# Shared experts of 512 tokens computed in pieces between the attention's steps

## The chip, the cores and the metric

The kernel runs on one core of a Trainium2 chip. A core has a matrix engine (TensorE, PE in the profile), VectorE (DVE), ScalarE (ACT), GpSimd (POOL) and SyncE (SP), each with an instruction stream of its own; they meet through semaphores. Data live in SBUF (128 partitions) and PSUM (the matmuls' accumulators), and DMA queues move them from and to HBM. The metric is the device time of one launch in microseconds (us): before the change the median of 8 runs is 1922.06 us (1921.56 to 1927.59).

## The reference

Four residual layers follow each other on x (1250 nodes of 512 values), each with a layer norm ahead of it. The change touches the first two; the two behind (a message passing layer with GRU and a KAN layer) only follow.

```python
x = x + gnn(layernorm(x), edges)           # attention over 21,250 edges, 8 heads of 32
x = x + ffn(layernorm(x))                  # router, 2 shared and 64 routed experts
x = x + gnn2(layernorm(x), edges, edge_attr)
x = x + kan(layernorm(x))

# gnn: att = exp(Q[receiver].K[sender]/sqrt(32)), normalised over a receiver's edges
out = relu(segment_sum(att * V[sender])); out = relu(out @ Wa + ba); out = relu(out @ Wf + bf)
return x + out
# ffn
shared = sum_over_2(silu(x @ Wg.T) * (x @ Wu.T) @ Wd.T) / 2
probs = softmax(x @ router_w.T + bias); top_p, top_i = top_k(probs, 6); top_p /= sum(top_p)
# each expert takes at most C = 234 of its tokens, in the order of the tokens
sparse = segment_sum(gate * (silu(t @ w_gate[e].T) * (t @ w_up[e].T)) @ w_down[e].T)
return shared + sparse
```

## The kernel before, in words

Tokens lie in ten tiles of 128 (`NT`), in chunks of 512, 512 and 256 (`CHUNKS`). `xr` keeps the residual stream in SBUF, `hT` the transposed normed tokens. The stages of the span, in us: counting of edges, norm, Q, K and V to 164; attention to 412; a tail to 444; shared experts of chunk 0 and the look-up of places to 491; shared experts of chunk 2 and the first experts' tokens to 515; routed experts to 991; shared experts of chunk 1 and the next norm to 1080; messages, GRU and KAN to the end. Matmuls in f32 are two PE instructions each.

**Attention.** Edges are counted into `cnts` (sender by receiver). A step is one chunk, one half of the heads and one tile b of ten senders: 3 chunks, 2 halves, 10 steps. `scores` (L472) makes four matmuls (L477) into two PSUM buffers `ps` (of three in all), takes the exponent on ACT into `ex` (L482) and multiplies it by the counts on DVE into `wt` (L484). `weighted` (L490) sums V and ones with it on PE (L496). The loop at L534 issues `scores` two steps ahead of `weighted`. After a half, `normalised` (L499) copies the sums to `s` on ACT, and DVE takes the reciprocal (L506) and writes `aggT` (L507).

**What is put between the steps.** At b = 5 of a chunk's first half, `output` (L510) of the chunk before runs whole: L517 and L525 on PE, and on DVE the bias into `o2` (L528; the profile calls it o) and the ReLU into `xr` (L530). Then the generator `route` (L386) gives one part behind each step: statistics of two tiles; `h` on ACT (L182), its transpose on PE (L191) and `hT` on ACT (L192) for each tile; router matmuls (L402) and softmax; top six (L418, L419); one-hot choices `hot` (L431); their sum `sel` (L435); the place of each choice in its expert's list, by matmuls on `sel` and `before` (L440, L441); `hu`, `pos` and `tat` (L449 to L456). The last part issues on POOL's queue one scatter (L459) for each tile and choice, which writes token and gate into the table `tokt` in HBM: 24 for a chunk of four tiles, 12 for the last chunk. The tail, L555 to L557, is `output` and `route` of the last chunk and what is left of the route before it.

**Behind the attention.** `sg` and `sd`, the weights of the shared experts (3 MB), are loaded by SP (L566 to L568) into memory that the attention's tiles held. `order` (L626) is the list of experts by load; SP reads it to address their weights. The program's dependencies let its write wait for the scatters. `shared_experts(*CHUNKS[0])` (L628) makes four pairs of gate and up matmuls (L582), Silu on ACT (L585), their product `sT` on DVE (L586), and for each tile the down matmuls (L590) and the sum into `xr` (L593). SP loads the table back as `tokb` (L631) when the last scatter has landed. Behind the last matmul of that call, `by_place` (L645) and `by_rank` sort the table by 42 small matmuls (L652, L658); `tok` (L676), `gate` and `goal` come from them. `shared_experts(*CHUNKS[2])` (L681) follows. `Tile.load` (L740) sends an expert's weights on SP into one of six buffers `w`, each load behind the one before it and the first behind `tokb`; `Tile.rows` (L750) gathers its tokens on POOL (L206) from `xtab`, to which the route has written `h`; `hidden` and `result` hold the expert matmuls (L764, L781). POOL adds each result to `acc` in HBM (L787). Chunk 1's shared experts run behind the routed experts.

**Memory.** Pools on SBUF's left side open and close in a stack, and pools on its right side in another.

Of the kernel before, what the change touches and what calls it, by code (L numbers as in the profile page):

```python
# [10 lines left out]
F32 = mybir.dt.float32  # L11
BF = mybir.dt.bfloat16
F16 = mybir.dt.float16
I16 = mybir.dt.int16
I32 = mybir.dt.int32
# [7 lines left out]
P = 128  # L23
N = 1250
NT = 10
# [54 lines left out]
def gnn_ffn_kernel(ctx: ExitStack, tc: tile.TileContext, a: dict, out: bass.AP):  # L80
# [21 lines left out]
    early = until_attended.enter_context(tc.tile_pool(name="early", bufs=1))  # L102
    srcf = early.tile([P, ET], F32, name="srcf")
    dstf = const.tile([P, ET], F32, name="dstf")
# [7 lines left out]
    with tc.tile_pool(name="near", bufs=1) as temp:  # L112
# [10 lines left out]
        nc.vector.tensor_reduce(n_far, near, AX.X, OP.add)  # L123
    iot_i = early.tile([P, P], I32, name="iot_i")
    nc.gpsimd.iota(iot_i, pattern=[[1, P]], base=0, channel_multiplier=0)
    iot = const.tile([P, P], F32, name="iot")
    nc.vector.tensor_copy(iot, iot_i)
    iotn = early.tile([P, NP], F16, name="iotn")
    with tc.tile_pool(name="iot_t", bufs=1) as temp:
# [92 lines left out]
    with tc.tile_pool(name="gat", bufs=1) as gw:  # L222
# [88 lines left out]
        with tc.If(far):  # L311
            with tc.tile_pool(name="gat_f", bufs=2) as work, \
                    tc.tile_pool(name="gat_fp", bufs=1, space=PSUM) as psum:
                for j in range(0, NT, 2):
# [10 lines left out]
                    for i in range(2):  # L325
                        nc.vector.scalar_tensor_tensor(
                            cnts[:, j + i], pc[i][:, :NP], 1.0, cnts[:, j + i], op0=OP.mult,
                            op1=OP.add, accum_out=deg[:, j + i:j + i + 1])

        wa = gw.tile([P, HD // P, D], F32, name="wa")  # L330
        nc.sync.dma_start(out=wa, in_=a["Wa"].rearrange("(c p) f -> p c f", p=P))
# [46 lines left out]
        nc.vector.scalar_tensor_tensor(qh, qe, -2.0, qf, op0=OP.mult, op1=OP.add)  # L378

        sel = rt.tile([P, NT, NE], BF, name="sel")  # L380
        before = rt.tile([P, NT + 1, NE], BF, name="before")
# [3 lines left out]

        def route(t0, n, work, psum):  # L386

# [4 lines left out]
            def new(name, *shape, dt=F32):  # L392
                return work.tile([P, n, *shape], dt, name=name, bufs=1)
# [53 lines left out]
            yield  # L447
            hu = new("hu", TOPK, NE)
            nc.vector.tensor_tensor(hu, hot, u[:, :, None, :].to_broadcast([P, n, TOPK, NE]), OP.mult)  # L449
# [5 lines left out]
            tat = work.tile([P, n, TOPK], I32, name="tat", bufs=2)  # L455
            nc.vector.tensor_scalar(tat, past, float(NPOS), None, op0=OP.add)  # L456
            for t in range(n):
                for k in range(TOPK):
                    s = nc.gpsimd.indirect_dma_start(  # L459
                        out=tokt, out_offset=IndirectOffsetOnAxis(ap=tat[:, t, k:k + 1], axis=0),  # L460
                        in_=entry[:, t0 + t, k], in_offset=None)
                    for other in scatters:
                        tc.declare_no_dep(s.ins, other.ins, reason="each place is of one choice")
                    scatters.append(s)

        with tc.tile_pool(name="gat_e", bufs=3) as work, \
                tc.tile_pool(name="gat_o", bufs=2) as owork, \
                tc.tile_pool(name="gat_r", bufs=1) as rwork, \
# [3 lines left out]
            def scores(n0, n, half, b):  # L472

                ps = [psum.tile([P, 2, 512], F32, name="ps") for _ in range(2)]
                for i in range(4):
                    q = slice(i * DK, (i + 1) * DK)
                    nc.tensor.matmul(ps[i // 2][:, i % 2, :n], KT[q, half, b * P:(b + 1) * P],  # L477
                                     QT[q, half, n0:n0 + n], start=True, stop=True)
                wts = []
                for p in ps:  # L480
                    ex = work.tile([P, 2, 512], F32, name="ex")
                    nc.scalar.activation(ex[:, :, :n], p[:, :, :n], AF.Exp, scale=DK ** -0.5)  # L482
                    wt = work.tile([P, 2, 512], F32, name="wt", bufs=6)
                    nc.vector.scalar_tensor_tensor(  # L484
                        wt[:, :, :n], ex[:, :, :n], HUGE,
                        cnts[:, b, None, n0:n0 + n].to_broadcast([P, 2, n]), op0=OP.min, op1=OP.mult)
                    wts.append(wt)
                return wts

            def weighted(n, half, b, wts, acc):  # L490

                for part in range(2):
                    for i in range(4):
                        h = 4 * half + i
                        v = ones[:, :DK] if part else V[:, b, h * DK:(h + 1) * DK]
                        nc.tensor.matmul(acc[part][i * DK:(i + 1) * DK, :n], v, wts[i // 2][:, i % 2, :n],  # L496
                                         start=b == 0, stop=b == NT - 1)
# [12 lines left out]
            def output(n0, n, aggT):  # L510
                o1T = owork.tile([P, DC, 512], F32, name="o1T", bufs=1)
                for f in range(0, DC, 2):
                    p1 = psum.tile([P, 2, 512], F32, name="ps")
                    for i in range(2):
                        fs = slice((f + i) * P, (f + i + 1) * P)
                        for c in range(HD // P):
                            nc.tensor.matmul(p1[:, i, :n], wa[:, c, fs], aggT[:, c, :n], start=c == 0,  # L517
                                             stop=c == HD // P - 1)
                        nc.scalar.activation(o1T[:, f + i, :n], p1[:, i, :n], AF.Relu,
                                             bias=cols[:, C_BA + f + i:C_BA + f + i + 1])  # L520
                for t in range(0, n // P, 2):
                    p2 = psum.tile([P, 2, D], F32, name="ps")
                    for i in range(2):
                        for c in range(DC):
                            nc.tensor.matmul(p2[:, i], o1T[:, c, (t + i) * P:(t + i + 1) * P], wf[:, c],  # L525
                                             start=c == 0, stop=c == DC - 1)
                    o2 = owork.tile([P, 2, D], F32, name="o2", bufs=1)
                    nc.vector.tensor_add(o2, p2, bf[:, None, :].to_broadcast([P, 2, D]))  # L528
                    xs = xr[:, n0 // P + t:n0 // P + t + 2]
                    nc.vector.scalar_tensor_tensor(xs, o2, 0.0, xs, op0=OP.max, op1=OP.add)  # L530

            steps = [(n0, n, half, b) for n0, n in CHUNKS for half in range(2) for b in range(NT)]
            ready, done, acc, aggT, parts = [], None, None, None, iter(())
            for i in range(len(steps) + 2):  # L534
                if i < len(steps):
                    ready.append(scores(*steps[i]))
                if i < 2:
                    continue
                n0, n, half, b = steps[i - 2]
                if b == 0:  # L540
                    acc = [psum1.tile([P, 512], F32, name=f"acc{k}") for k in range(2)]
                    if half == 0:
                        aggT = owork.tile([P, 2, 512], F32, name="aggT")
                weighted(n, half, b, ready.pop(0), acc)
                if b == NT // 2 and half == 0 and done:
                    output(*done)
                    parts = chain(parts, route(done[0] // P, done[1] // P, rwork, psum))
                    done = None
                else:
                    next(parts, None)  # L550
                if b == NT - 1:
                    normalised(n, half, acc, aggT)
                    if half == 1:
                        done = n0, n, aggT
            output(*done)  # L555
            for _ in chain(parts, route(done[0] // P, done[1] // P, rwork, psum)):
                pass  # L557
# [3 lines left out]

    until_moe = ExitStack()
    shared = until_moe.enter_context(tc.tile_pool(name="shared", bufs=1, reuse_waits="tile"))
    sg = shared.tile([P, 2, DC, 2 * FF], F32, name="sg")
    sd = shared.tile([P, 2 * FF // P, D], F32, name="sd")
    for i in range(2):  # L566
        nc.sync.dma_start(out=sg[:, i], in_=a["shared_in"][i].rearrange("(c p) f -> p c f", p=P))
    nc.sync.dma_start(out=sd, in_=a["shared_out"].rearrange("(c p) d -> p c d", p=P))  # L568
    until_edges = ExitStack()
# [27 lines left out]
    with tc.tile_pool(name="moe", bufs=1, side="right") as mw, tc.tile_pool(name="moe_w", bufs=6) as ew:  # L597
        with tc.tile_pool(name="moe_s", bufs=1) as keep, \
# [28 lines left out]

            last = shared_experts(*CHUNKS[0], keep, psum, psum1)  # L628

# [50 lines left out]
            goals(goal.rearrange("p r h -> p (r h)"), pm[:, 2])  # L680
            shared_experts(*CHUNKS[2], keep, psum, psum1)  # L681


# [196 lines left out]
    finishing.close()  # L880
    until_edges.close()
    until_msgs.close()
    until_moe.close()


    with ExitStack() as kan:
# [281 lines left out]
        def new(name, bufs):  # L1168
            return work.tile([P, 2, KC], F32, name=name, bufs=bufs)
# [231 lines left out]
```

## Time and profile before

| | us |
|---|---|
| Median of 8 runs | 1922.06 |
| Profiled execution, its own time | 1922.51 |
| Its span | 1920.8 |
| PE busy | 1815.2 |
| DVE, ACT, POOL busy | 1030.6, 756.7, 441.6 |
| Third norm transpose of chunk 1's route | starts 380.42 |
| Last `weighted` step ends, first L517 of the last chunk | 407.1 |
| First slot matmul of chunk 2 (L440) | 443.46 |
| Scatters of chunk 1, of chunk 2 | 412.4 to 442.2, 448.3 to 463.2 |
| `tokb` issued | 465.46 |
| First gather of an expert's tokens | 494.39 |
| First expert transpose, first expert matmul | 514.30, 515.78 |

A time in this table is a start on its engine from the span's beginning, unless it says otherwise. Busy times of engines overlap, so they do not add up to the span. A stage's own numbers say more than the whole span's: in a window, the idle time of PE is the window's length less its busy time, and the granted clock tells whether busy time was at full speed. A wait is put down to the instruction whose end released it.

### The profile page before, as it was taken

The numbers are of one execution on the slowest core, as the hardware profiler recorded it, in microseconds if no ns is written. First come the engines' busy times: TensorE is split into PE (matmuls) and PEld (weight loads), VectorE is DVE, ScalarE is ACT, GpSimd is POOL, SyncE is SP. The second block draws the span as 40 slices with busy tenths as digits, with TensorE's granted clock in tenths as the row PEclk, the third lists the DMA queues.
The fourth block names the chain that finished last, engine by engine and source line by source line (L and its number), as shares of the span: only waits on it lengthen the run. The fifth ranks groups of instructions, "written<-read, shape, count | busy, mean of one in ns | idle before, by whom it ended". The sixth has DMA issues, their size and how long they took to land. (4 is left out here: it accounts for less than half of the span.)

```text
span 1920.8 us, 20622 instructions
## 1 busy us (share of the span) xinstructions
PE 1815.2 (95%) x7477; PEld 898.3 (47%) x7477; DVE 1030.6 (54%) x1742; ACT 756.7 (39%) x1193; POOL 441.6 (23%) x421
## 2 busy tenths in 40 slices
PE   6999998968999999999989899998999999998999
PEld 4664232334544444444434334333447766664644
DVE  8765859563111111111128365552235987899995
ACT  3214644421022222222212144441116877687772
POOL 0000000434134444444420377761000000000000
PEclk9999999988999999999999999999999999999999
DMA  8000000004399999888864488881110001000000
GB/s 316 5 1 2 1 17 7 23 3 179 130 272 302 279 308 291 246 305 300 296 157 138 130 283 283 287 284 48 49 49 1 1 33 62 5 11 1 11 10 22
DMA packets 68403, 247.24 MB, mean 129 GB/s; under 512 B 11889, under 2 KB 14705, under 8 KB 59189
## 3 DMA queue, kind: packets, MB, share of 16 engines
q1 hardware_dynamic: 29954, 147.65, 20.5%
q0 software_dynamic: 32656, 83.97, 16.6%
q10 hardware_dynamic: 5666, 14.05, 2.0%
q8 instruction: 66, 1.08, 0.2%
q14 instruction: 61, 0.49, 0.1%
HBM read 210.23 MB, written 35.39 MB: 128 GB/s over the span
## 5 line engine op out<-in xcount | busy, mean ns | idle before, releaser
L764 PE MATMUL pg<-w,xT 128*128 128x512 f32 (+4 forms) x752 | 274.9, 595 | 3.9 <-DMA w<-in_experts 3.0
L768 DVE TENSOR_TENSOR gs<-gs,pg 128x256 f32<-128x256 f32 (+2 forms) x76 | 32.0, 421 | 390.6 <-ACT gs L767 390.6
L206 POOL DMA_INDIRECT hg<-ptab,srci x167 | 158.3, 948 | 153.3 <-DVE at L974 90.1
L764 PEld LDWEIGHTS pg<-w,xT 128*128 128x128 f32 (+4 forms) x752 | 105.3, 164 | 161.0 <-issue 158.4
L787 POOL DMA_INDIRECT acc<-y,goal x94 | 140.6, 1495 | 155.5 <-ACT y L785 134.8
L932 PE MATMUL pm<-w1e,eat 128*128 128x512 f32 x334 | 159.1, 614 | 8.8 <-DVE m L934 8.0
L781 PE MATMUL py<-w,gT 128*128 128x512 f32 (+4 forms) x376 | 149.4, 611 | 9.6 <-ACT gT L776 3.3
L1237 PE MATMUL pk<-basis,w1s 128*128 128x256 f32 x640 | 150.0, 381 | 2.1 <-DVE basis L1219 2.1
L1260 PE MATMUL py<-block,basis 128*128 128x512 f32 x320 | 142.8, 607 | 9.3 <-DVE basis L1219 9.3
L934 DVE TENSOR_TENSOR m<-pm,hg 128x1024 f32<-128x1024 f32 x84 | 102.3, 1218 | 83.6 <-PE pm L932 46.7
L935 ACT ACTIVATE m<-m 128x1024 f32<-128x1024 f32 x84 | 88.1, 1050 | 137.2 <-DVE m L934 137.2
L1237 PEld LDWEIGHTS pk<-basis,w1s 128*128 128x128 f32 x640 | 120.1, 190 | 39.8 <-issue 14.8
L1196 DVE SCALAR_TENSOR_TENSOR cube<-held,knots,sq 128x512 f32<-128x512 f32 x180 | 135.3, 754 | 4.4 <-ACT sq L1192 4.1
L1192 ACT ACTIVATE sq<-held,negk 128x512 f32<-128x512 f32 x180 | 127.4, 710 | 24.3 <-DVE cube L1196 24.2
L482 ACT ACTIVATE ex<-ps 128x1024 f32<-128x1024 f32 (+1 forms) x120 | 101.1, 883 | 88.0 <-PE ps L477 65.7
L484 DVE SCALAR_TENSOR_TENSOR wt<-ex,cnts 128x1024 f32<-128x1024 f32 (+1 forms) x120 | 119.6, 1041 | 28.2 <-ACT ex L482 28.2
L767 ACT ACTIVATE gs<-pg 128x256 f32<-128x256 f32 (+2 forms) x76 | 29.1, 383 | 223.6 <-PE pg L764 210.2
L785 ACT ACTIVATE y<-py,gate 128x512 f32<-128x512 f32 (+2 forms) x76 | 52.2, 686 | 159.4 <-PE py L781 122.4
L206 POOL DMA_INDIRECT xg<-xtab,tok x76 | 75.0, 987 | 159.4 <-PE pt L758 121.5
L932 PEld LDWEIGHTS pm<-w1e,eat 128*128 128x128 f32 x334 | 60.0, 192 | 99.2 <-issue 77.0
L1260 PEld LDWEIGHTS py<-block,basis 128*128 128x128 f32 x320 | 62.2, 196 | 86.8 <-issue 71.4
L1203 ACT ACTIVATE right<-cube 128x512 f32<-128x512 f32 x135 | 84.0, 622 | 39.5 <-DVE cube L1196 35.4
(284 smaller groups left out, 2736.4 us busy)
## 6 DMA issues: line engine op xcount, KB each, us to landing
w<-in_experts SPq DMA_DIRECT2D x64, 1536.0 KB, 10.5
eat<-in_edge SPq DMA_DIRECT2D x20, 512.0 KB, 5.8
acc<-zero SPq DMA_DIRECT2D x33, 256.0 KB, 5.1
part<-acc SPq DMA_DIRECT2D x30, 256.0 KB, 5.3
block<-in_w SPq DMA_DIRECT2D x3, 1536.0 KB, 6.2
w1s<-in_w1s ACTq DMA_DIRECT2D x4, 1024.0 KB, 4.9
block<-in_Wih ACTq DMA_DIRECT2D x4, 768.0 KB, 6.8
block<-in_Whh ACTq DMA_DIRECT2D x4, 768.0 KB, 6.4
```

The costliest lines, as they stand in the source:

```text
L206: nc.gpsimd.indirect_dma_start(out=dst, out_offset=None, in_=table, in_offset=IndirectOffsetOnAxis(ap=at, axis=0))
L482: nc.scalar.activation(ex[:, :, :n], p[:, :, :n], AF.Exp, scale=DK ** -0.5)
L484: nc.vector.scalar_tensor_tensor(wt[:, :, :n], ex[:, :, :n], HUGE, cnts[:, b, None, n0:n0 + n].to_broadcast([P, 2, n]), op0=OP.min, op1=OP ...
L764: nc.tensor.matmul(ph[p0:p0 + n], xT[:, c, p0:p0 + n], weights[r][:, c:2 * DC:DC], start=c == 0, stop=c == DC - 1)
L781: nc.tensor.matmul(py[p0:p0 + n], gT[:, f, p0:p0 + n], weights[r][:, k:k + 2].rearrange("p a b -> p (a b)"), start=f == 0, stop=f == 1)
L787: nc.gpsimd.indirect_dma_start(out=next(turn), out_offset=IndirectOffsetOnAxis(ap=self.goal[:n, r, h:h + 1], axis=0), in_=y[p0:p0 + n], in ...
L932: firsts.append(nc.tensor.matmul(pm[:, i], eat_t, w1e, start=True, stop=True))
L934: nc.vector.tensor_add(m[:, :k], pm[:, :k], hg[:, :k])
L1192: nc.scalar.activation(self.sq[k], self.x, AF.Square, bias=negk[:, k:k + 1])
L1196: nc.vector.scalar_tensor_tensor(self.cube[k], self.x, knots[:, k:k + 1], self.sq.pop(k), op0=OP.subtract, op1=OP.mult)
L1237: nc.tensor.matmul(pk[o], w[:, o * P:(o + 1) * P], b[:, c], start=half == 0 and g == 8 and c == 0, stop=half == 1 and g == 7 and c == 1)
L1260: nc.tensor.matmul(py[m], b[:, c, m * P:(m + 1) * P], w, start=g == 8 and c == 0, stop=g == 7 and c == 1)
```

## The change

Nine edits come together.

1. Two tiles of constants and the sources of the edges, needed only while edges are counted, move from the pool `early` to a pool on the right side that is closed after the counting; constants of the routing, which take that place, are therefore made after it.
2. `sg` and `sd` are placed on the right side and loaded ahead of the attention, behind the stores that clear `acc`.
3. `ex` goes: the exponent is written into `wt`, and DVE multiplies in place. `o2` goes: the bias is added in place in PSUM. `hu` becomes 16-bit.
4. Chunk 0's route takes two parts a step for b = 6 to 8 of chunk 1's first half, so it ends three steps earlier. Its 24 scatters are issued in eight pieces of three, each with a conversion of three places of its own, behind the newest product of the steps (`issue_after`). Routes of the other chunks keep one conversion and one piece.
5. `normalised` is issued ahead of what is put behind a step.
6. `shared_pair`, a generator, computes the shared experts of two tiles in six pieces. Two pairs, tiles 0 to 3, form `fill`: a piece stands behind each step of the last chunk's second half (ten), and the rest is issued in turns with the parts of the tail.
7. Behind the attention chunk 2's shared experts take the place of chunk 0's, and nothing stands where chunk 2's stood. The cast of `order` stays ahead of them.
8. `output` is a generator, since its parts alternate with `fill` in the tail.
9. `until_moe` closes ahead of `until_msgs`.

```diff
@@ counting, loads
-    srcf = early.tile([P, ET], F32, name="srcf")
+    until_counted = ExitStack()
+    counting = until_counted.enter_context(tc.tile_pool(name="counting", bufs=1, side="right"))
+    srcf = counting.tile([P, ET], F32, name="srcf")
...
+        until_moe = ExitStack()
+        shared = until_moe.enter_context(tc.tile_pool(name="shared", bufs=1, side="right"))
+        sg = shared.tile([P, 2, DC, 2 * FF], F32, name="sg")
+        sd = shared.tile([P, 2 * FF // P, D], F32, name="sd")
+        for i in range(2):
+            nc.sync.dma_start(out=sg[:, i], in_=a["shared_in"][i].rearrange("(c p) f -> p c f", p=P))
+        nc.sync.dma_start(out=sd, in_=a["shared_out"].rearrange("(c p) d -> p c d", p=P))
@@ route
-            nc.vector.tensor_scalar(tat, past, float(NPOS), None, op0=OP.add)
-            for t in range(n):
-                for k in range(TOPK):
+            pieces = [(t, k, TOPK // 2) for t in range(n) for k in (0, TOPK // 2)] if behind else [(0, 0, n * TOPK)]
+            places, from_ = (x.rearrange("p t k -> p (t k)") for x in (tat, past))
+            for t, k0, m in pieces:
+                at = slice(t * TOPK + k0, t * TOPK + k0 + m)
+                with tc.issue_after(behind().ins) if behind else nullcontext():
+                    nc.vector.tensor_scalar(places[:, at], from_[:, at], float(NPOS), None, op0=OP.add)
+                for i in range(at.start, at.stop):
...
+                yield
@@ scores
-                    ex = work.tile([P, 2, 512], F32, name="ex")
-                    nc.scalar.activation(ex[:, :, :n], p[:, :, :n], AF.Exp, scale=DK ** -0.5)
-                    wt = work.tile([P, 2, 512], F32, name="wt", bufs=6)
-                    nc.vector.scalar_tensor_tensor(
-                        wt[:, :, :n], ex[:, :, :n], HUGE,
+                    wt = work.tile([P, 2, 512], F32, name="wt")
+                    nc.scalar.activation(wt[:, :, :n], p[:, :, :n], AF.Exp, scale=DK ** -0.5)
+                    newest[:] = [nc.vector.scalar_tensor_tensor(
+                        wt[:, :, :n], wt[:, :, :n], HUGE,
@@ output
-                    o2 = owork.tile([P, 2, D], F32, name="o2", bufs=1)
-                    nc.vector.tensor_add(o2, p2, bf[:, None, :].to_broadcast([P, 2, D]))
+                    nc.vector.tensor_add(p2, p2, bf[:, None, :].to_broadcast([P, 2, D]))
                     xs = xr[:, n0 // P + t:n0 // P + t + 2]
-                    nc.vector.scalar_tensor_tensor(xs, o2, 0.0, xs, op0=OP.max, op1=OP.add)
+                    nc.vector.scalar_tensor_tensor(xs, p2, 0.0, xs, op0=OP.max, op1=OP.add)
+                    yield
+
+            def shared_pair(t0):
+                ts = slice(t0 * P, (t0 + 2) * P)
+                sT = owork.tile([P, 2 * FF // P, 2 * P], F32, name="sT")
+                for i in range(2):
+                    p = psum.tile([P, 2 * FF // P, 2 * P], F32, name="ps")
+                    for f in range(2 * FF // P):
+                        for c in range(DC):
+                            nc.tensor.matmul(p[:, f], sg[:, i, c, f * P:(f + 1) * P], hT[:, c, ts],
+                                             start=c == 0, stop=c == DC - 1)
+                        if f == 1:
+                            yield
+                    if i == 0:
+                        nc.scalar.activation(sT, p, AF.Silu)
+                    else:
+                        nc.vector.tensor_mul(sT, sT, p)
+                    yield
+                p = psum.tile([P, 2, D], F32, name="ps")
+                for i in range(2):
+                    for f in range(2 * FF // P):
+                        nc.tensor.matmul(p[:, i], sT[:, f, i * P:(i + 1) * P], sd[:, f], start=f == 0,
+                                         stop=f == 2 * FF // P - 1)
+                    if i == 0:
+                        yield
+                xs = xr[:, t0:t0 + 2]
+                nc.vector.scalar_tensor_tensor(xs, p, 0.5, xs, op0=OP.mult, op1=OP.add)
+                yield
@@ the loop over steps
+            fill = chain(shared_pair(0), shared_pair(2))
...
+                if b == NT - 1:
+                    normalised(n, half, acc, aggT)
                 if b == NT // 2 and half == 0 and done:
-                    output(*done)
-                    parts = chain(parts, route(done[0] // P, done[1] // P, rwork, psum))
+                    for _ in chain(parts, output(*done)):
+                        pass
+                    first_tile, k = done[0] // P, done[1] // P
+                    parts = route(first_tile, k, rwork, psum, None if first_tile else lambda: newest[0])
                     done = None
                 else:
-                    next(parts, None)
...
+                    for _ in range(2 if n0 == CHUNKS[1][0] and half == 0 and b < 9 else 1):
+                        next(parts, None)
+                if n0 == CHUNKS[2][0] and half:
+                    next(fill, None)
...
-            output(*done)
-            for _ in chain(parts, route(done[0] // P, done[1] // P, rwork, psum)):
+            for _ in zip_longest(chain(output(*done), parts, route(done[0] // P, done[1] // P, rwork, psum)), fill):
                 pass
@@ behind the attention
             order = mw.tile([1, NE], I32, name="order")
             nc.vector.tensor_copy(order, po)
-            last = shared_experts(*CHUNKS[0], keep, psum, psum1)
+            last = shared_experts(*CHUNKS[2], keep, psum, psum1)
...
             goals(goal.rearrange("p r h -> p (r h)"), pm[:, 2])
-            shared_experts(*CHUNKS[2], keep, psum, psum1)
```

## The prediction, made before the change was run

> **What bounds the kernel now.** I read the page's first two parts, then busy time by stage around the edit, then what TensorE (PE) waits for there, then the order of time on PE, and last the transfers that the edit exposes.
>
> ```profile
> PE 1815.2 (95%) x7477; PEld 898.3 (47%) x7477; DVE 1030.6 (54%) x1742; ACT 756.7 (39%) x1193; POOL 441.6 (23%) x421
> ```
>
> PE is busy 95% of the span, so an edit that leaves its work alone can win only from its idle time and its slow stretches. The stages by window (us from the span's start; busy time and instructions of each engine, PE's granted clock, DMA share):
>
> ```profile
> 250.00:345.00 95.00, 85.44 (x589) 30.92 (x586) 70.39 (x100) 45.35 (x61) 12.55 (x15) 0.96 0.04 12
> 345.00:380.00 35.00, 31.30 (x172) 13.56 (x175) 15.05 (x27) 13.68 (x23) 14.73 (x16) 1.00 0.05 16
> 380.00:412.00 32.00, 25.31 (x265) 13.26 (x255) 27.50 (x60) 11.66 (x22) 1.08 (x2) 0.89 0.05 18
> 412.00:444.00 32.00, 17.31 (x56) 11.45 (x57) 14.14 (x56) 7.68 (x12) 24.56 (x26) 0.67 0.18 55
> 444.00:491.00 47.00, 44.98 (x103) 19.41 (x103) 10.40 (x36) 3.67 (x5) 11.86 (x13) 0.94 0.62 247
> 491.00:515.00 24.00, 23.95 (x129) 17.78 (x128) 4.72 (x14) 1.53 (x4) 2.91 (x3) 1.00 0.12 34
> ```
>
> The end of the attention (380 to 412) and its tail (412 to 444) leave PE idle for 6.7 and 14.7 us at clocks of 0.89 and 0.67. From 444 on PE is full: there the shared experts hide the table's way to the first expert. What PE waits for from 412 to 516 (total us, times, longest):
>
> ```profile
> PE ps L191 <- ACT h L182: 8.4, 1, 8.4
> PE ps L440 <- DVE sel L435: 6.2, 1, 6.2
> PE ps L517 <- DVE aggT L507: 2.7, 1, 2.7
> PE pu L582 <- DVE sT L586: 1.6, 1, 1.6
> ```
>
> DVE there has one wait that PE hardly feels, for the table's entries, and SP's queue hangs on the same event:
>
> ```profile
> DVE order L626 <- DMA tokt<-entry,tat: 10.3, 1, 10.3
> ```
> ```profile
> 465.46 0.34 SPq L631 DMA_DIRECT2D tokb<-tokt  x1
> 467.38 70.90 SPq L748 DMA_DIRECT2D w<-in_experts  x8
> ```
>
> The timeline of PE shows the price of an idle stretch:
>
> ```profile
> 385.50 3.79 PE L402 MATMUL ps<-rw,hT 128*128 128x64 f32 x32
> ...
> 431.80 1.97 PE L191 MATMUL ps<-ident,h 128*128 128x128 f32 x8 [8.40 <-ACT h L182]
> 433.60 3.67 PE L402 MATMUL ps<-rw,hT 128*128 128x64 f32 x16
> ```
>
> After 8.4 us of idling, 16 router matmuls take what 32 took before. The same happens after a stall of 2.87 us at 315.9, and not after 2.19 or 2.64: I count half speed for 4 to 6 us after a stall of 2.9 us or more. The gather of an expert tile, issue to landing (min/median/max over 76):
>
> ```profile
> DMA to landing us min/median/max: 3.2/5.6/15.7
> ```
>
> The experts themselves (516 to 991) are 97% PE, and wait for weights only this long:
>
> ```profile
> PE pg L764 <- DMA w<-in_experts: 3.0, 4, 0.9
> ```
>
> So shifting the start of the experts shifts everything behind it.
>
> **The change part by part.** The sum is made on the profiled execution (span 1920.8, time 1922.51; the median of the runs is 1922.06, 0.45 lower).
>
> *Work moved on PE.* A pair of tiles of the shared experts is four pieces of 16 instructions of 256 columns (chunk 2's L582 shows 1.73 for 8: 3.46) and two of 8 of 512 columns (0.43 each: 3.43), 20.7 us; two pairs are 41.4, what chunk 0's call costs now. Nothing is removed.
>
> *End of the attention, plus 24.6.* From the third norm transpose (380.42) to the last `weighted` (407.09) are 26.7 us, 18.7 of them work (7 `scores` of 0.64, 9 `weighted` of 1.0, router matmuls 3.79, two transposes of 0.6, slot matmuls). Nine pieces now stand there: 7 x 3.46 + 2 x 3.43 = 31.1. The 8 us of stalls and slow clock (1.70 on `sel`, 1.13 on `before`, 1.11 on `wt`, the half-rate steps after 403) are filled; I leave 1.5 for a multiply of sT queued behind `sel` (2.75) on DVE. 18.7 + 31.1 + 1.5 = 51.3. Range 23.1 (no stall) to 29.7 (all of two Silu and two Exp table loads on ACT showing, 1.28 each as at L585; ACT is busy 11.7 of 32, so I count none).
>
> *The tail, plus 1.9.* The tail runs from there to the first slot matmul, X (L440, 443.46): 36.4 us, bound by the chain aggT, output, norm, router, sel. One piece now covers the wait for aggT (2.74 back), one of 3.43 stands ahead of L525, and the add into xr of 1.22 ahead of the norm on DVE: 3.43 + 1.22 - 2.74. At best a warm clock also returns 3.2 us (L517's 16 instructions take 6.7 there, 3.46 at full speed): -1.3; at worst the wait is no gain: +4.7.
>
> *From X to the first expert matmul, minus 29.9.* Now 72.3 (443.46 to 515.78), with 41.2 + 20.6 of shared experts. After, only chunk 2's 256 tokens stay, and part of their pu matmuls runs ahead of X: 15.5 to 18 us. The table sets the end: the 12 scatters of chunk 2 (448.3 to 463.2, 1.26 each on POOL) land at X + 22.0 as now. The cast of `order` waits for them on DVE, and the fourth multiply of sT is now queued behind it; five of the eight down matmuls wait for that one. (Now it is the second multiply of chunk 0 that waits, at a cost of 1.6.) So: multiply done at X + 22.7; PE has idled some 5 us, and its 4.3 us of matmuls take 6.5 with the slow start; by_place to gather 3.6 (490.8 to 494.39), and 1.0 for the slow clock; landing 5.6; transpose to expert matmul 1.5 (514.30 to 515.78), 1.5 more at half speed: X + 42.4. Bounds: landing 3.4 as now and full clock, X + 35.5 (-36.8); landing 15.7 and half clock throughout, X + 54.6 (-17.7). The weights issue at X + 23.9 as now; the first load lands 7.0 to 17.2 later, median 8.9, ahead of X + 42.4 but for the longest. SP's six free buffers hold 9.4 MB, 22 us at the 428 GB/s of that stretch, so the first gathers now share the DMA engines with them; now they start when the loads have landed.
>
> [...]
>
> *Chunk 0's route pulled forward, plus 1.5.* Two parts a step in b = 6 to 8 put two transposes (0.6 each) and the router matmuls (3.7) ahead of the end of half 0 of chunk 1: at most 4.9 later for `normalised`, at 289.0 now. From there DVE is nearly full until 337, and it loses the 1.63 us that it waits for L402 at 302. Between -1.6 (that alone) and +4.9, I take near the middle. The scatters in pieces of three put 8 instead of 1 conversions of 0.17 on DVE; POOL, busy 12.6 of 95 us, covers the 30 us of scatters, and only entries of chunk 2 are awaited last.
>
> *In-place bias add, plus 1.0.* A PSUM buffer is held through L528 and L530 (1.22 each) instead of the first: 0 to 1.22 for each of five pairs of tiles, 0 to 6.1; most have two other buffers free. ex written into wt costs 0 while its six buffers last (three steps of two); a step short would show as a wait of L477 on DVE, 0.3 (its L482 wait now 0.4).
>
> *Loads and constants, plus 0.5.* sg and sd (3 MB) go out at about 41 us, at the end of the page's first slice; the next shows 5 GB/s: 0 (10 us at 316 GB/s if the counting stage needed the queue, and nothing there does). Seventeen small constants move from the first 5 us to about 160, where DVE idles 9.3 us: -1 to 0. Behind the experts w1e (now 1045.8) waits for the ptab writes and a memset of 4.33 (now 1047.4) follows the last pv; the first message add waits for its gather until 1088.9 anyway: 0 to 4.3, taken 0.5 with the constants.
>
> Sum: 24.6 + 1.9 - 29.9 + 1.5 + 1.0 + 0.5 = -0.4, 1921.7 beside the median. What is won in the attention's idle time (6.5) and tail is lost again where the table's latency lies bare (about 5 at `order`, 6 to 9 at the gather).
>
> **The rivals.**
> - *Faster, by a warm clock.* If PE still has work when `order` comes, its stall stays under 2.9 us and no half rate follows. That needs X + 19.8 or more of work; 20.6 if none of chunk 2's shared work ran ahead of X, against my 15.5 to 18. The tail's idle stretches filled speak for it, too. Then the tail is -1.3 and the rest 22.7 + 4.3 + 3.6 + 5.6 + 1.5 = 37.7, -34.6: sum -8.3, 1913.8.
> - *Slower, by the first gather.* It starts at X + 33, inside the 22 us of weight loads. At the 15.7 that a gather has taken, the sum is +9.7, 1931.8. It decides from a landing of 9.8 us, where the sum passes +3.8. The median of 5.6 under weight loads speaks against it; that all buffers load at once only here speaks for it.
> - *Nothing moves.* If the pieces drained in the tail instead of between the steps, they would fill its 14.7 idle us alone and the end would be near the old one. The written order of PE speaks against it.
>
> **How the numbers follow.** A measurement of this kernel tells 0.2% (3.8 us) from no change. The forecast has 0.45, its own range -8 to +8 by the spread of chunk 1 (6.5) and the tail (6.0), so 0.13 faster, 0.18 same, 0.14 slower. The warm clock has 0.25, all faster; the gather 0.28, all slower; nothing moved 0.02, same. Together 0.38, 0.20, 0.42. The range reaches a little past the two rivals, 1910 to 1935.
>
> **What would show it.** Right: PE without waits over 1.5 us from 380 to the last `weighted`, some 24 us later than now; X 26 to 30 later; PE waiting some 5 us on sT behind `order`, then 6 us or more on the gather; the experts starting within 8 us of 515.8 and lasting 475 as now. Wrong: a wait of `scores` on PSUM or ACT inside the filled steps, a gather beyond 10 us, no stall at `order`, or a difference behind 991.

## The result, and the profile after

The changed kernel takes 1928.37 us (median of 12 runs, 1926.05 to 1932.69), the one before 1923.54 (35 runs beside it): a ratio of 1.0028, with a 95% interval from 1.002 to 1.0036. It is slower by some 5 us, where the forecast was no change. The profiled execution's span went from 1920.8 to 1925.8, so its trace holds the whole difference, and the same marks can be read in both traces (starts in us; the last column is the part of the difference that arose since the mark above):

| mark | before | after | later by | arose here | predicted |
|---|---|---|---|---|---|
| third norm transpose of chunk 1's route | 380.42 | 381.70 | 1.3 | 1.3 | 2.5 |
| PE done with the last `weighted` | 407.09 | 434.27 | 27.2 | 25.9 | 24.6 |
| first slot matmul of chunk 2 (X) | 443.46 | 472.06 | 28.6 | 1.4 | 1.9 |
| first expert matmul | 515.78 | 516.67 | 0.9 | -27.7 | -29.9 |
| last sum of the norm stage (pv) | 1079.97 | 1081.21 | 1.2 | 0.3 | 0 |
| first message add | 1088.94 | 1094.73 | 5.8 | 4.6 | 0.5, constants included |
| end of the span | 1920.8 | 1925.8 | 5.0 | -0.8 | 0 |

Around the edit itself things went much as worked out. Busy time by stage of the changed kernel (columns as in the prediction):

```profile
380.00:412.00 32.00, 30.41 (x231) 21.33 (x232) 17.92 (x43) 12.38 (x20) 1.08 (x2) 1.00 0.05 17
412.00:444.00 32.00, 32.00 (x209) 20.92 (x208) 14.17 (x19) 9.50 (x15) 9.64 (x10) 1.00 0.01 1
444.00:491.00 47.00, 38.27 (x129) 25.82 (x127) 21.33 (x85) 7.32 (x12) 25.37 (x28) 0.82 0.06 14
491.00:517.00 26.00, 11.17 (x66) 6.93 (x66) 3.66 (x12) 0.00 (x0) 4.67 (x5) 0.73 0.81 308
```

From 380 to 444 PE now idles for 1.6 us where it idled for 21.4, at full clock. In return it idles for 23.6 us from 444 to 517, at 0.82 and 0.73, where it had been full. What it waits for from 444 to 517:

```profile
PE pt L804 <- DMA xg<-xtab,tok: 11.2, 2, 8.8
PE ps L193 <- ACT h L184: 5.4, 1, 5.4
PE py L638 <- DVE sT L634: 3.7, 1, 3.7
PE ps L455 <- DVE sel L450: 2.9, 1, 2.9
```

The gathers (first row) and the product queued behind `order` (third) are the waits that the prediction named; the tail's two (second and fourth) have shrunk from 8.4 and 6.2. On PE's timeline the end of this stretch reads:

```profile
494.83 6.25 PE L638 MATMUL py<-sd,sT 128*128 128x512 f32 x10 [3.67 <-DVE sT L634]
500.92 1.14 PE L700 MATMUL pt<-moved,tokb 128*128 128x60 f32 x20
...
512.46 1.09 PE L804 MATMUL pt<-ident,xg 128*128 128x128 f32 x4 [8.81 <-DMA xg<-xtab,tok]
515.90 0.98 PE L804 MATMUL pt<-ident,xg 112*128 112x112 f32 x4 [2.35 <-DMA xg<-xtab,tok]
516.67 8.65 PE L810 MATMUL pg<-w,xT 128*128 128x512 f32 x16
```

The loss lies 560 us further on, at the first messages, in code that the change doesn't touch. POOL's, DVE's and PE's timelines there, before the change:

```profile
1083.80 1.07 POOL L206 DMA_INDIRECT hg<-ptab,srci  x1 [90.09 <-DVE at L974]
1085.17 0.99 POOL L206 DMA_INDIRECT hg<-ptab,srci  x1 [0.30 <-issue]
```
```profile
1047.43 4.33 DVE L921 MEMSET rT<- 128x5120 f32 x1 [1.01 <-issue]
...
1079.97 0.69 DVE L877 TENSOR_TENSOR pv<-pp,b 128x512 f32<-128x512 f32 x1 [2.74 <-PE pp L875]
...
1088.94 1.22 DVE L934 TENSOR_TENSOR m<-pm,hg 128x1024 f32<-128x1024 f32 x1 [4.42 <-DMA hg<-ptab,srci]
```
```profile
1080.72 3.70 PE L932 MATMUL pm<-w1e,eat 128*128 128x512 f32 x8 [0.79 <-DVE pv L877]
```

and after it, first POOL, then DVE, then PE:

```profile
1085.15 5.52 POOL L208 DMA_INDIRECT hg<-ptab,srci  x1 [90.54 <-issue]
1090.97 0.99 POOL L208 DMA_INDIRECT hg<-ptab,srci  x1 [0.30 <-issue]
```
```profile
1081.21 0.69 DVE L923 TENSOR_TENSOR pv<-pp,b 128x512 f32<-128x512 f32 x1 [2.74 <-PE pp L921]
1085.18 4.33 DVE L967 MEMSET rT<- 128x5120 f32 x1 [3.28 <-issue]
...
1094.73 1.22 DVE L980 TENSOR_TENSOR m<-pm,hg 128x1024 f32<-128x1024 f32 x1 [3.69 <-DMA hg<-ptab,srci]
```
```profile
1087.44 6.59 PE L978 MATMUL pm<-w1e,eat 128*128 128x512 f32 x8 [6.26 <-DMA w1e<-in_W]
```

Two things are new, side by side. PE waits 6.26 us for w1e, which SP sends out at 1084.29 where it did at 1045.82. And the first message gather, whose issue on POOL took 1.07 us, takes 5.52, while DVE zeroes rT beside it, a memset that ran 37.8 us earlier before the change; the message add waits for that gather and the next. Either can be the cause, or both. The first experiment took it to be w1e.

### The profile page after: what moved, and what is told of

Read it like the earlier page. It is cut to its first block, busy times and chain, and to the rows that moved or that the text cites. A ratio compares the mean times of both kernels' runs of the same rounds, so it can differ in the third digit from the quotient of the medians.

```text
span 1925.8 us, 20764 instructions
## 1 busy us (share of the span) xinstructions
PE 1821.1 (95%) x7541; PEld 914.3 (47%) x7541; DVE 1031.3 (54%) x1745; ACT 759.4 (39%) x1194; POOL 447.6 (23%) x421
## 5 line engine op out<-in xcount | busy, mean ns | idle before, releaser
L208 POOL DMA_INDIRECT hg<-ptab,srci x167 | 162.9, 975 | 152.4 <-issue 130.4
L504 DVE SCALAR_TENSOR_TENSOR wt<-wt,cnts 128x1024 f32<-128x1024 f32 (+1 forms) x120 | 120.0, 1040 | 42.0 <-ACT wt L503 41.9
L503 ACT ACTIVATE wt<-ps 128x1024 f32<-128x1024 f32 (+1 forms) x120 | 99.4, 880 | 105.3 <-PE ps L498 101.0
```

What stands on the lines that cost most here:

```text
L208: nc.gpsimd.indirect_dma_start(out=dst, out_offset=None, in_=table, in_offset=IndirectOffsetOnAxis(ap=at, axis=0))
L504: newest[:] = [nc.vector.scalar_tensor_tensor(wt[:, :, :n], wt[:, :, :n], HUGE, cnts[:, b, None, n0:n0 + n].to_broadcast([P, 2, n]), op0=O ...
```

## The experiments

The runs below were on chips on which the kernel before takes 1996 to 1998 us. On them engines stand still now and then where the trace shows nothing that they wait for; such a gap on DVE, in the tail of the first run:

```profile
481.64 1.23 DVE L549 TENSOR_TENSOR ps<-ps,bf 128x1024 f32<-128x1024 f32 x1 [25.69 <-remote]
```

Gaps like this fall in different places in different kernels (8.57 us up to 1143.94 in the run of the late load alone, 4.54 up to 1128.72 in the third run of half of the fill, both on DVE), so a ratio between two kernels there says less than its interval suggests. The verdicts on the message stage and on the stretch from X to the first expert matmul therefore rest on lengths inside one trace, without such a gap between the marks.

**Unused memory ahead of the late pools.** The first theory was w1e. The place of w1e in SBUF had belonged to `sg`, free before the norm stage ended; after the change the pools of the norm stage lie there, so that the load waits for all ptab writes.

```diff
     finishing = ExitStack()
+    spacer = finishing.enter_context(tc.tile_pool(name="spacer", bufs=1))
+    spacer.tile([P, 12288], mybir.dt.uint8, name="spaced")
     late = finishing.enter_context(tc.tile_pool(name="moe_l", bufs=1, reuse_waits="tile"))
```

> The changed kernel with 12 KB per partition of unused memory ahead of the pools that follow the experts, so that w1e lies where no tile of the norm and ptab stage lies, and its load goes out between the ptab writes as it did before the change. Nothing else moves. Theory: the 5 us that the change loses come from this load. In the changed kernel the first message matmul waits 6.3 us for w1e, starts 6.7 us later than before the change and runs at half clock, and the second is 5.8 later, where the end of the norm stage was only 1.2 later: so 4.6 of it goes, and the kernel stands within 1 us of the one before (0.9 later at the first expert matmul). Rival: the message adds wait for their gathers anyway, and the loss was made by the moved shared experts; then it stays 4 to 5 us slower than before.

Measured: 1.0003 of the kernel before (0.9992 to 1.0014). To set the changed kernel beside it on one chip, both ran again, twice.

> The changed kernel as it is, once more, so that the next two runs stand beside it on one chip: the three runs before this came from a chip on which the kernel before takes 1996 us. Expected 0.2 to 0.36% slower than before, as measured first. If this chip should show no loss, the load of w1e isn't what made it on the first.

> The changed kernel with the unused 12 KB ahead of w1e, once more beside it. Theory (the load of w1e): 4 to 5 us faster than the changed kernel in the same rounds, within 1 us of the one before. Rival: no difference between the two, and the earlier ratio of 1.0003 was a matter of that chip.

> The changed kernel beside the others of this call. Expected 0.25 to 0.5% slower than the kernel before, as in its first two measurements (1.0028, 1.0047).

> The changed kernel with the memory ahead of w1e, beside it on one chip. Theory: 4 to 5 us faster than the changed kernel. Earlier ratios to the kernel before were 1.0003 and 1.0031 on a chip with stray waits of some 12 us; by the traces it should be 0.5 to 2 us slower than before. Rival: what is left beside w1e is over 3 us.

Measured on the second chip: changed 1.0047 (1.0031 to 1.0062), with the memory 1.0031 (1.0019 to 1.0042). On the third: changed 1.0043 (1.0027 to 1.006), with the memory 1.0001 (0.9989 to 1.0013). So the changed kernel is slower on every chip that it ran on, and the unused memory takes the loss away on one and a third of it on another. I put the scatter down to the gaps; that is not shown. The lengths in the traces agree better: from the last pv to the first message add it is 13.4 to 13.5 us in each run of the changed kernel, and 8.8 to 9.2 with the memory. But 12 KB shift all tiles of the norm stage, off the place of rT as well as off that of w1e, and DVE's memset is early again too (1081.03 in the third chip's run). The expectation's "nothing else moves" was wrong: the experiment undoes the loss in the message stage, and does not tell which of the two made it.

**The late load alone,** in the kernel before.

```diff
-            nc.sync.dma_start(out=ptab[t * P:(t + 1) * P], in_=pv)
+            stored = nc.sync.dma_start(out=ptab[t * P:(t + 1) * P], in_=pv)
...
-            nc.sync.dma_start(out=w1e, in_=a["W1"][D:])
+            with tc.issue_after(stored.ins):
+                nc.sync.dma_start(out=w1e, in_=a["W1"][D:])
```

> The kernel before the change, with one difference: the load of w1e goes out on SP behind the last ptab write, not between the first two. Theory: that order alone costs 2 to 4 us (0.1 to 0.2%): issued near 1081, landed some 3 later, so that the first message matmul waits 3 to 4 us and runs at half clock, where it had waited 0.8. It is less than in the changed kernel, because this load doesn't wait for the writes to land. Rival: the message add waits for its gather until 1088.9 anyway, and nothing is lost: within 1 us.

Measured: 0.9994 (0.9982 to 1.0006). PE waits for w1e, as meant, yet the message add is not later. PE's timeline, then POOL's:

```profile
1116.43 8.00 PE L933 MATMUL pm<-w1e,eat 128*128 128x512 f32 x12 [4.43 <-DMA w1e<-in_W]
```
```profile
1115.97 1.02 POOL L206 DMA_INDIRECT hg<-ptab,srci  x1 [91.70 <-DMA w1e<-in_W]
```

From the last pv (1112.03) to the first message add (1120.94) it is 8.9 us, as without the late load: the add waits for its gather in any case. So a late load need not cost anything, and the theory's 2 to 4 us for it fell. But this load goes out 1.1 us after the last pv (1113.17), the changed kernel's 3.1 after it (1084.29), so a small share of w1e in the loss is still possible. What this run shares with the kernel before is the gather of 1 us and a memset made long ahead of it (at 1079.49).

**The late memset alone,** in the kernel before, made twice because the changed kernel's starts 2 us later, counted from the last pv, than this one can.

```diff
-            nc.vector.tensor_add(pv, pp, b1)
+            summed_pv = nc.vector.tensor_add(pv, pp, b1)
...
-            nc.vector.memset(rT, 0.0)
+            with tc.issue_after(summed_pv.ins):
+                nc.vector.memset(rT, 0.0)
+                nc.vector.memset(rT, 0.0)
```

> The kernel before the change, with the memset of rT issued on DVE behind the last sum of the norm stage, and made twice (2 x 4.33 us), so that it still runs when POOL issues the first gather of messages, as in the changed kernel. The load of w1e goes out early, as before. Theory (new): a memset on DVE holds up the gather that POOL issues beside it; the gather's 1.07 us become 4 to 6, ending about 1.2 after the memset, and the first message add comes 5 to 6 us later: 0.2 to 0.3% slower. Rival (the first theory): the loss was w1e's load; then the gather takes 1 us, DVE is ready in time, and nothing is lost: within 0.1%.

Measured: 1.002 (1.0004 to 1.0036). POOL's timeline, and DVE's:

```profile
1115.84 3.37 POOL L206 DMA_INDIRECT hg<-ptab,srci  x1 [90.11 <-issue]
1119.52 5.09 POOL L206 DMA_INDIRECT hg<-ptab,srci  x1 [0.30 <-issue]
1124.91 0.95 POOL L206 DMA_INDIRECT hg<-ptab,srci  x1 [0.30 <-issue]
```
```profile
1113.72 4.33 DVE L922 MEMSET rT<- 128x5120 f32 x1 [1.01 <-issue]
...
1119.34 4.33 DVE L923 MEMSET rT<- 128x5120 f32 x1 [1.02 <-issue]
...
1127.23 1.22 DVE L936 TENSOR_TENSOR m<-pm,hg 128x1024 f32<-128x1024 f32 x1 [3.48 <-DMA hg<-ptab,srci]
```

Two memsets, two held gathers. The first gather ends 1.16 us after the first memset does (1119.21 and 1118.05), and in the changed kernel the same sum gives 1.16 too (1090.67 and 1089.51); the second ends 0.94 after the second memset. That is about a whole gather's time (1.07 and 0.99), so it gets next to nothing done while the memset runs. The gather after the second memset is back at 0.95. The first add comes 15.2 us after the last pv, 6.2 later than in the kernel before, as expected, and the rival (nothing lost) falls.

**The memset off DVE,** in the changed kernel, whose load of w1e stays late.

```diff
-            nc.vector.memset(rT, 0.0)
+            nc.scalar.activation(rT.rearrange("p c (t k) -> p (c t) k", k=P),
+                                 iot[:, None, :].to_broadcast([P, DC * NT, P]), AF.Copy, scale=0.0)
```

> The changed kernel, with rT zeroed by ACT (a copy with scale 0) in place of DVE's memset; the load of w1e stays as late as in the changed kernel, behind the landings of the ptab writes. Theory: the first message gather takes 1 us on POOL although w1e is late and ACT is busy beside it, and 4 to 5 us of the changed kernel's loss go: within 0.1% of the kernel before. Rival (w1e): PE still waits 6 us for w1e and nothing is won: 0.3 to 0.47% slower than before.

Measured: 1.0007 (0.9991 to 1.0023). ACT zeroes rT in 4.47 us, and POOL's gather beside it takes 1.02:

```profile
1116.88 4.47 ACT L967 ACTIVATE rT<-iot 128x5120 f32<-128x5120 f32 x1 [9.80 <-issue]
```
```profile
1117.76 1.02 POOL L208 DMA_INDIRECT hg<-ptab,srci  x1 [90.16 <-DVE at L1021]
```

From the last pv to the first add it is now 10.4 us, of 13.5 in the changed kernel and 9.0 before: 3.2 us of the 4.6 are the memset's, less than the 4 to 5 expected. The 1.4 left stand beside the late w1e. The first add needs four PE instructions behind that load:

```profile
1119.87 3.75 PE L979 MATMUL pm<-w1e,eat 128*128 128x512 f32 x4 [6.09 <-DMA w1e<-in_W]
```

They end at 1123.62, so the add could not start before 9.8 us after the last pv, 0.8 later than in the kernel before, whatever the gathers do. (In the changed kernel the same four end 3.5 us ahead of the add, and the wait for w1e is covered.) The rest lies in the gathers' landing, which comes last: the add starts 5.1 us after the second gather's issue (1119.08), and 3.8 after it in the kernel before. Why they land later here is not shown; the load of w1e, issued at 1116.90, moves beside them.

**The change without the moved shared experts,** on top of the unused memory.

```diff
-            fill = chain(shared_pair(0), shared_pair(2))
+            fill = iter(())
...
-            last = shared_experts(*CHUNKS[2], keep, psum, psum1)
+            last = shared_experts(*CHUNKS[0], keep, psum, psum1)
...
+            shared_experts(*CHUNKS[2], keep, psum, psum1)
```

> The kernel with the memory ahead of w1e, and the shared experts where they were before the change: chunk 0's behind the attention, chunk 2's behind the look-up of places, no pieces between the steps. What stays of the change is the route of chunk 0 pulled forward with its scatters in threes, the in-place products and bias adds, the early loads and the later constants. Theory: these cost what the changed kernel's third norm transpose of chunk 1 shows, 1.3 us; 1 to 1.5 slower than before. Rival: the pieces between the steps hide something that these edits cost elsewhere, and it is 4 or more slower; or they gain in the tail (early weights, PE order), and it is faster.

Measured: 1.001 (1.0001 to 1.0019), beside 1.0003 for the memory alone on that chip. So what stays of the change costs 0.2 to 3.8 us, which holds the expected 1 to 1.5 and leaves the rival (4 or more, or faster) out, and the fill neither gains nor loses by itself beyond the interval. The gaps fall differently in the two kernels, so this is the weakest of the verdicts, and which of the edits costs it is not separated.

**The cast of order behind the shared experts' sums,** on top of the unused memory.

```diff
             order = mw.tile([1, NE], I32, name="order")
-            nc.vector.tensor_copy(order, po)
             last = shared_experts(*CHUNKS[2], keep, psum, psum1)
+            with tc.issue_after(added[-1].ins):
+                nc.vector.tensor_copy(order, po)
```

(`added` lists the sums into `xr` that `shared_experts` issues.)

> The kernel with the memory ahead of w1e, and besides the cast of order issued on DVE behind the sums of the last chunk's shared experts, no longer ahead of their fourth product. Theory: PE's wait of 3.7 us for sT and the half clock behind it go; the look-up of places can start when tokb lands, about 496.2 instead of 500.9, so everything from there is 4 to 5 us earlier than with the memory alone, 3 to 4 us faster than before the change. Rival: the gathers land when the weight loads leave room, not a fixed time behind their issue; the loads keep their place in time, so the first expert starts less than 1.5 us earlier.

Measured: 0.9983 (0.9974 to 0.9992), against 1.0003 without this edit. PE's timeline:

```profile
529.44 1.68 PE L703 MATMUL pt<-moved,tokb 128*128 128x60 f32 x20 [1.92 <-DMA tokb<-tokt]
...
542.05 1.09 PE L807 MATMUL pt<-ident,xg 128*128 128x128 f32 x4 [8.54 <-DMA xg<-xtab,tok]
```

The look-up now starts with the table's landing, 25.4 us after X, where it started at 28.9. Of these 3.5, 2.5 reach the first expert matmul (42.1 after X against 44.6): the look-up runs at half clock (0.53 granted from 529.4 to 534; 1.68 for what took 1.14), and the gather takes 7.6 us, of 7.9 in the changed kernel. That is less than the 4 to 5 us expected there, and more than the rival's 1.5.

**The gathers ahead of the weights,** on top of the unused memory: a row of each gathered tile is copied to HBM on SP before the first weight load, which therefore waits for the landing.

```diff
...
+                    if i == 0 and loads == [landed]:
+                        for first in tiles[:2]:
+                            first.rows()
+                        for first in tiles[:2]:
+                            loads.append(nc.sync.dma_start(out=probe, in_=first.x[0:1]))
                     if i < len(tiles):
                         tiles[i].load()
...
```

> The kernel with memory ahead of w1e, in which the first two gathers of tokens go first, and SP copies a row of each to HBM before the first weight load, so that no weights move while they land. Theory: the gathers of the changed kernel (7.8 and 11.2 us from issue to landing) are slowed by the six weight loads under way; here they land in 3.4 to 4.5 us as before the change. The experts then wait for weights instead, and the kernel is 0 to 4 us slower than with the memory alone. Rival: the first gathers are slow for another reason, and land in 7 us or more here too.

One execution, with a profile. POOL issues the first gather at 538.85, and PE has it 3.4 us later:

```profile
542.24 1.08 PE L806 MATMUL pt<-ident,xg 128*128 128x128 f32 x4 [4.29 <-DMA xg<-xtab,tok]
543.71 0.98 PE L806 MATMUL pt<-ident,xg 112*128 112x112 f32 x4 [0.39 <-DMA xg<-xtab,tok]
```

In the changed kernel it is 7.9 (504.56 to 512.46), behind six weight loads issued from 495.95 to 501.60, of which the first had landed (502.67). So the loads make the difference, and the gather lands within the expected 3.4 to 4.5 us once they are held back; the rival falls. It doesn't pay: PE then stands 10.0 us before the first expert matmul, which comes 48.7 us after X, against 45.8 with the memory alone on that chip (2008.34 us in this one run, against a median of 2003.43).

**Half of the fill,** with both edits above: tiles 0 and 1 in pieces, the last three steps and the tail taking them, tiles 2 and 3 behind the look-up of places.

```diff
-            fill = chain(shared_pair(0), shared_pair(2))
+            fill = shared_pair(0)
...
-                if n0 == CHUNKS[2][0] and half:
+                if n0 == CHUNKS[2][0] and half and b > 6:
...
             goals(goal.rearrange("p r h -> p (r h)"), pm[:, 2])
+            shared_experts(256, 256, keep, psum, psum1)
```

> The kernel with the memory ahead of w1e and the cast of order behind, and with only tiles 0 and 1 in pieces: three behind the last three steps, three in the tail. Tiles 2 and 3 run behind the look-up of places. Theory: the full fill wins 14 us of PE's idle time (5 between the steps, 9 in the tail: 31.1 of work cost 25.9, 10.3 cost 1.4) and loses 14 behind the first slot matmul, because no work is left to hide the way from the table to the gathered tokens. Half of the work is enough for the tail, and the other half hides the gather: 8 to 10 us faster than before. Rival: what the fill wins is lost again behind it whichever work is moved, since the last scatter sets the end; then within 3 us of before.

> The kernel with memory ahead of w1e, order behind, and half of the fill, once more, on a chip shared with the changed kernel. Theory: 8 to 10 us faster than before (0.5%), as on the other chip, and 13 to 15 faster than the changed kernel. Rival: a part of the 0.5% was made by that chip's long waits in the tail; then 3 to 6 us faster.

> Memory ahead of w1e, order behind, tiles 0 and 1 in pieces, tiles 2 and 3 behind the look-up of places. Theory: 5 to 10 us faster than before (ratios of 0.995 and 0.9969 so far). Rival: on a chip without the stray waits nothing of it is left: within 2 us.

Measured: 0.995 (0.9932 to 0.9968), 0.9969 (0.9948 to 0.9989) and 0.9948 (0.9931 to 0.9966): 6 to 10 us faster than before on three chips, and faster than the changed kernel on both chips that ran the two together. What PE waits for in the third of these runs from 495 to 540, all of it:

```profile
PE pt L703 <- DMA tokb<-tokt: 1.5, 1, 1.5
PE py L640 <- issue: 0.3, 1, 0.3
```

The wait for the gather is gone: the 23 us of tiles 2 and 3 (510.11 to 533.38), with the gathers issued at 511.25, cover it. The expectation holds in direction; in size it holds on the first and third chip (10 us each), while the 6.2 us of the second lie between theory (8 to 10) and rival (3 to 6). The rivals of the first and third run, within 2 or 3 us of before, fall.

## Why the prediction was wrong

The forecast was 1922, no change; the kernel lost 0.28%, more than the 0.2% that it counted as no change. Its chances gave slower 0.42, but 0.28 of that for a first gather of 9.8 us or more, and the loss came from elsewhere: that the likeliest sign came true is luck. The table at the head shows where the terms stand.

- *End of the attention* (24.6, measured 25.9) and *tail* (1.9, measured 1.4): right. The wait left on sT was 1.59, against 1.5. ACT's table loads there for Silu and Exp (1.28 us each, at 388.70, 392.58 and 424.95) showed in no other wait of PE from 380 to 434.
- *From X to the first expert matmul* (-29.9, measured -27.7): right in its mechanism, at both places. The stall behind `order` was 3.67, not some 5, and the ten instructions behind it took 6.25 as against 6.5. The gather was issued 32.5 us after X, where the terms give 33.8, but landed in 7.9, not 5.6; the second took 10.0 and held PE for 2.35 more. The median of all gathers was the wrong row: it counts gathers beside one load or two (58 loads of 10.5 us in the median, issued from 531.8 to 975.8 in the kernel before), and these were issued behind six, as the rival said. The rival's own point (9.8 us) was not reached by the first gather; the second passed it. Of the terms that were off, this is the second in size, 2.2 us.
- *Chunk 0's route, in-place add* (2.5 together, measured 1.3 up to chunk 1's third transpose): within the stated bounds; the two are not separated, and not all of the five bias adds lie ahead of that mark.
- *Behind the experts* (0 to 4.3, taken 0.5): this is the step that failed. It said of the late w1e and the late memset that "the first message add waits for its gather until 1088.9 anyway", and so took both as covered. For the memset that is wrong, since the gather is what the memset holds up: the cover was not independent of what it covered. The stretch grew by 4.6 us, 3.2 of them the memset's. For w1e it holds only as long as the gather is late: with the memset off DVE the other 1.4 stay, 0.8 of which PE's product behind w1e makes by itself; what delays the gathers for the rest is open. With 0.9 from the edit's own place, and small differences of +0.3 and -0.8 ahead of and behind this stretch, that is the loss.

The rivals: neither the warm clock nor the gather decided, and none named the message stage as a place where the sign is made. "A difference behind 991" stood at the end of the prediction among what would make it wrong, and it did. The clock after `order` fell as assumed (0.50 granted from 497 to 499, 1.00 from 500 on), so the warm-clock rival failed at its condition: PE ran dry 19.1 us after X (472.06 to 491.16), against the 15.5 to 18 that I had counted and the 19.8 that the rival needed.

## What to carry to other kernels

A change of where tiles lie in memory moves instructions in code that nobody edited: compare the order on each engine over the whole kernel, and cost each moved instruction with the engines it disturbs, not only with its own wait. When one edit removes a loss, list everything that it moved before naming the cause; here it took the late load and the late memset tried one by one. Work used to fill idle time may have been the cover of a latency elsewhere: move only as much as that latency can spare.

## What the runs showed of the hardware that was not expected

The gathers that POOL issued while DVE ran its memset of 128 x 5120 f32 (4.33 us) got next to nothing done until it ended: 5.52 us in place of 1.07 in the changed kernel (at 1085.15, and at 1118.96 in its third run), and 3.37 and 5.09 beside two such memsets. ACT, writing the same tile in 4.47 us, left the gather at 1.02.

The clock also fell to half after shorter waits than the 2.9 us that I had counted. In the third run of the half fill, PE's timeline after a wait of 1.48 us:

```profile
506.81 1.25 PE L703 MATMUL pt<-moved,tokb 128*128 128x60 f32 x20 [1.48 <-DMA tokb<-tokt]
507.99 0.69 PE L709 MATMUL pt<-moved,tokb 128*128 128x128 f32 x2
508.47 1.71 PE L703 MATMUL pt<-moved,tokb 128*128 128x60 f32 x20
510.11 3.78 PE L632 MATMUL pg<-hT,sg 128*128 128x256 f32 x8
...
516.06 1.89 PE L632 MATMUL pg<-hT,sg 128*128 128x256 f32 x8
```

Eight instructions take 3.78, and 1.89 some 6 us later. My bound of 2.9 us came from waits of 2.19, 2.64 and 2.87; here the wait is followed by 42 matmuls of 2 to 128 columns, and whether these had a part in it was not tried. The kernel before already spoke against the bound: around eight slot matmuls PE waits 1.70 and 1.13 us (401.53 and 402.92), and from 404 to 407 the granted clock is 0.50. Nor did the length of a wait decide alone. The same transposes behind the same wait, first in the changed kernel, then in the first run with the unused memory, which changes nothing there:

```profile
376.62 1.11 PE L193 MATMUL ps<-ident,h 128*128 128x128 f32 x4 [2.08 <-ACT h L184]
```
```profile
393.51 0.66 PE L193 MATMUL ps<-ident,h 128*128 128x128 f32 x4 [2.08 <-ACT h L184]
```

The granted clock behind the first is 0.50 (376.6 to 378), behind the second 1.00 (393.5 to 394.9).
